# A convolution-attention hybrid on one core: an earlier second chunk, statistics beside their sums, and a reordered first tile

## The chip, the core and the metric

The kernel runs on one NeuronCore of a Trainium2 chip. A core has a matrix engine (TensorE, PE in the profile; its weight loads are PEld), a vector engine (VectorE, DVE), a scalar engine (ScalarE, ACT), a general engine (GpSimd, POOL) and a queue processor that only issues DMAs (SyncE, SP). Each works through its own instruction stream in order and waits on semaphores for the others. Matrix products land in PSUM[...]; everything else is in SBUF. The metric is the device time of one launch in microseconds (us). The comparison uses the median of several runs; the profile is one more, separate execution.

## What is computed

The input is four images of 32 x 128 x 128 in f32. Layer 0 is self-attention inside an image: the image is cut into 2 x 2 blocks, which gives 128 channels by 4096 positions, and each position attends to all the others. Layer 1 takes the result as 4 x 4096 tokens of width 128 and adds a linear attention and a routed layer of eight experts.

```python
def _L0_conv_ref(x, gamma):
    ...
    q = xs.reshape(B, C * R * R, hw)
    energy = jnp.einsum('bci,bcj->bij', q, q)
    d = jnp.sqrt(jnp.diagonal(energy, axis1=1, axis2=2))
    energy = energy / (d[:, :, None] * d[:, None, :])
    attn = jax.nn.softmax(energy, axis=-1)
    out = jnp.einsum('bcj,bij->bci', q, attn).reshape(B, C * R * R, h, w)
    out = gamma * out + xs
    ...
def _L1_attn_ref(x, Wk, Wq, Wv):
    ...
    KtV = jnp.einsum('bhnk,bhne->bhke', K, V)
    out = jnp.einsum('bhnk,bhke->bne', Q, KtV)
def _L1_ffn_ref(x, router_w, router_b, expert_w, expert_b):
    router_probs = jax.nn.softmax(x @ router_w + router_b, axis=-1)
    top_p, top_i = jax.lax.top_k(router_probs, K)
    top_p = top_p / jnp.sum(top_p, axis=-1, keepdims=True)
    expert_out = jnp.einsum('bnd,edc->bnec', x, expert_w) + expert_b
    ...
t = t + _L1_attn_ref(_ln_t(t), ...)
t = t + _L1_ffn_ref(_ln_t(t), ...)
```

So `q` is a 128 x 4096 matrix for each image, `energy` is 4096 x 4096 and symmetric, each of its columns scaled to unit length before the softmax.

## The kernel before

**The attention of layer 0.** The 4096 positions are eight chunks of 512 (`NCH`), each of four blocks of 128 (`NJ`). `attend` (from line 474) goes through the rows of chunks, i = 0 to 7, and in a row through jc = 0 to i, and for each pair through four tiles j. Only the half of the symmetric matrix up to the diagonal is computed by TensorE. A tile is: one product `pe` of two chunks of normalised positions `qn` (line 609), its exponential `pr` on ScalarE with its row sum (line 612), and two tiles later the product `po` of `pr` with the values `qT` (line 497, the function `values`). All `po` products of a row add up in one PSUM bank, the only one of its pool; after the row's last one ScalarE copies the bank to `o` (line 502).

The other half comes by transposing: VectorE turns the 32 x 32 squares of `pr` into a buffer `F` (line 421; line 565 on the diagonal), SyncE sends `F` to memory (`blocks`, line 530, or `below`, line 554) and brings it back with its groups exchanged (`swap_groups`, six DMAs, line 545). A *transposed share* (`transposed_share`, line 433, and `diagonal_share`, line 453) then multiplies `F` with the values into a `pg` bank in four steps (two on the diagonal); ScalarE takes the row sums of `F` (lines 438 and 457), and VectorE adds `pg` to `o` (lines 442 and 462). Shares wait in the list `late` with a due time on `clock`, a count of matmul work: 57 units (`LAG`) after their loads are issued. `step_share` does one step if the first of them is due. `after(n, f)` puts `f` on a list of things that are due n tiles later; `turn_tick` carries out what is due. In each tile the order is: `pe`, exponential, `turn_tick` (so also `po`), `step_share`.

**Streams beside it.** In the loop over the images (line 1496) `attend` is run as a generator that yields twice a tile. At the first of the two yields the loop collects which side streams are to move: those in `timed`, which have a begin and an end in hundredths of the image's matmul work and a number of steps, and those in `steady`, which move once in 10 clock units (`PACE`). What was collected moves at both yields. From `manual_schedule` on, the order of PE, DVE, ACT and SP is the order in which the program issues; POOL is not in that list, but instructions marked `pinned` keep their order there.

**Preparing a chunk pair.** `prep` (two chunks at a time, kc = 0 to 3) loads the pair by `load_quarters` (four DMAs on line 308, into the pool `xin`, which has one buffer) and for image 0 the same part of the token layout `T` (`load_tokens`, line 279), turns it (`turn_quarters`, line 316, two VectorE transposes for each chunk), squares and sums it (`squares`, lines 295 and 296), takes the power -0.5 on POOL (`pow_neg_half`, line 164), spreads the result (`wide`, line 388), transposes that on PE (`pnorm`, line 399) and scales `T` by it to `qn` (line 372). `prep_first` does image 0's first pair in another way: it scales the turned values (`qs`, line 338) and transposes them on PE (`ptn`, line 344); 40 idle transposes on PE (`keep_running`, line 186) run while the loads are under way.

**Layer 1.** `layer1` follows an image one image later, beside the next one's attention. `attention_rows(u)` (line 943) handles eight token groups, four instances three stream steps apart: it turns the rows, adds the attention products three at a time (`pat`, lines 855 and 920), takes the statistics of the sums (`batch_stats`, `bn_stats` on VectorE, line 962), closes them (`close_stats`: six small VectorE operations, lines 682 to 688, then on POOL the power, line 164, and two products, lines 690 and 692, the last giving `nbo`), computes the router's rows, stores the sums (`t2`, line 970) and normalises on ScalarE (line 696), which reads `nbo`. The last image does this in `last_parts` instead.

Of the kernel before, what the change touches and what calls it, by code (L numbers as in the profile page):

```python
# [12 lines left out]
F32 = mybir.dt.float32  # L13
# [3 lines left out]
ALU = mybir.AluOpType  # L17
AX = mybir.AxisListType
# [4 lines left out]
def kernel(  # L23
# [43 lines left out]
    nc = tc.nc  # L67
    P = 128
# [3 lines left out]
    CH = 512  # L72
# [228 lines left out]

    def load_quarters(b, kc, queues=(nc.sync, nc.sync)):

        xa = xin.tile([P, 2, 2, 2, HW2, 2], F32, tag="xx", name=f"xa_{b}_{kc}")
        halves = x[b].rearrange("c (s g) w -> c s (g w)", s=2)
        for a in (0, 2, 1, 3):
            first_row = 16 * kc + 4 * a
            queues[a // 2].dma_start(
                xa[ts(a, S)].rearrange("p s k r w e -> p s (k r w e)"),
                halves[:, :, first_row * W : (first_row + 4) * W],  # L310
            )
        return xa

    def turn_quarters(s, xa, qT):
        for k in range(2):
            nc.vector.transpose(
                qT[:, s, 2 * k : 2 * k + 2, :].rearrange("p h (e r c) -> p r (h e) c", e=2, r=2),
                xa[:, s, k].rearrange("p r (h t) e -> p (r h) e t", h=2),
            )

    def prep_first(st):

        b, kc = 0, 0
        st["T"] = big1.tile([P, KT, D], F32, tag="T", name="T_0")
        xa = load_quarters(b, kc, (nc.sync, nc.scalar))
        qT = chunks_of(b, kc, st)
        yield
        ss = stat.tile([P, 2 * NJ], F32, tag="ss", name=f"ss_{b}_{kc}")
        rn = stat.tile([P, 2 * NJ, 1], F32, tag="rn", name=f"rn_{b}_{kc}")
        for s in range(2):  # L330
            turn_quarters(s, xa, qT)
            squares(b, kc, s, qT, ss)
            pow_neg_half(rn[:, ts(s, NJ), 0], ss[:, ts(s, NJ)])
        keep_running(40, ps_g, "pg")
        scaled = []
        for s in range(2):
            qs = work.tile([P, NJ, P], F32, tag="qs", name=f"qs_{b}_{kc}_{s}", bufs=2)
            nc.vector.tensor_tensor(qs, qT[:, s], rn[:, ts(s, NJ)].to_broadcast([P, NJ, P]), ALU.mult)
            scaled.append(qs)
        for s, qs in enumerate(scaled):  # L340
            qn = channels(b, kc, s, st)
            pt, done = hold(f"ptn_{b}_{kc}_{s}", lambda p, qn=qn: nc.scalar.activation(qn, p, AF.Copy))  # L342
            for j in range(NJ):
                nc.tensor.transpose(pt[:, ts(j, P)], qs[:, j, :], ident)
            done()
            yield

    def prep(b, kc, st):

        ahead = 2 if b == 0 and kc == 1 else 5
        xa = load_quarters(b, kc)
        if b == 0:
            load_tokens(st["T"][:, ts(kc, 8), :], b, 8 * kc, 8)
            xx = rows_of_image(b, kc, st)
        for _ in range(ahead):
            yield
        qT = chunks_of(b, kc, st)
        for s in range(2):  # L360
            turn_quarters(s, xa, qT)
            yield
# [26 lines left out]
        yield  # L389
        if b:  # L390
            yield

# [19 lines left out]

    def after(ticks, f):
        queued.append((tick[0] + ticks, f))

    def turn_tick():

        due = [f for at, f in queued if at <= tick[0]]
        queued[:] = [q for q in queued if q[0] > tick[0]]
        for f in due:  # L420
            f()  # L421

# [51 lines left out]
    def attend(b, st):  # L474
# [11 lines left out]
        for i in range(NCH):  # L486
# [94 lines left out]
            for jc in order:  # L581
# [21 lines left out]
                for j in range(NJ):  # L603
# [11 lines left out]
                    if ending and jc == order[-1] and j == NJ - 1:  # L615
                        st["exps"] = True
                    after(2, partial(values, pr[:, c0:], t, c0, CH))
                    if jc < i and not both:
# [8 lines left out]
                    elif jc == i and j in (1, 2):  # L627

                        after(1 if j == 2 and order[-1] == i else 2, partial(below, own, (2, 1) if j == 1 else (3,)))
                    turn_tick()  # L630
                    clock[0] += 2 * (CH - c0) // P
                    step_share()
                    yield

# [19 lines left out]
    def layer1(b, st):  # L654
# [288 lines left out]
        def attention_rows(u):  # L943
# [8 lines left out]
            yield  # L952
            la = stat.tile([P, 8, 2 * E], F32, tag="la", name=f"la_{b}_{u}")
            for j0 in range(0, 8, 3):
                yield
# [3 lines left out]
                done()  # L959
            bs, stats = batch_stats("f", 8 * u, 8)  # L960
            for j in range(8):
                stats[j]()
                if j == 3:
                    yield
                    yield
            logits = router_rows(nc.vector, 8 * u, 8, la)
            close_stats("f", 8 * u, 8, bs)
            next(logits)
            yield
            nc.sync.dma_start(t2[:, ts(u, 8)], T[:, ts(u, 8), :])  # L970
            yield
# [514 lines left out]
    first, second = prep_first(states[0]), prep(0, 1, states[0])  # L1486
    next(first)
    load_weights()
    next(first)
    next(second)  # L1490
    load_tokens(states[0]["T"][:, 0:8, :], 0, 0, 8)

    ordered = ExitStack()
    ordered.enter_context(tc.manual_schedule(engines=ENGINES))
    timed = [(first, 0, 1, 2), (second, 0.5, 5.5, 10)]
    for b in range(B):
# [82 lines left out]
```

## Time and profile before

Three runs took 1643.99, 1644.94 and 1645.40 us; the median is 1644.94. The profiled execution took 1638.94 us by itself.

| | us |
|---|---|
| median of the runs | 1644.94 |
| the profiled execution | 1638.94 |
| its span, first to last instruction | 1637.1 |
| PE busy | 1598.4 |
| DVE busy | 942.7 |
| ACT busy | 877.2 |
| POOL busy | 593.8 |

The mean granted clock of TensorE is 0.996 of full speed. DMA moves 345.18 MB, 211 GB/s over the span; the share of busy time of the DMA engines lies at 0.4 to 0.7 in the first image and at 0.7 to 0.9 in the following ones.

A line of the time line gives the start, the duration from the start of the first to the end of the last of the instructions merged in it, the engine, the line of the kernel, the operation, what is written from what, the shapes and the count; in brackets stands how long the engine was idle before it, and what ended that. A line of the waits gives who waited for whom, the total in us, how many times, and the longest. The ends of matmuls are modelled: a 512-wide f32 product is two instructions that start 0.43 us apart and are shown with 0.59 us each, so two products in a row overlap in the listing, and losses are better read from starts.

The chain that ended last is PE for 84% of the span: lines 497 (25%), 609 (24%) and 433 (21%) are the three kinds of products of the attention.

### The profile page before, as it was taken

Reading aid. Unit: us, or ns where it says so; the run is one execution under the profiler, and the core shown is the slowest. Engines: PE = TensorE matmul, PEld = TensorE weight load, DVE = VectorE, ACT = ScalarE, POOL = GpSimd, SP = SyncE. Lnnn points to the kernel's source line nnn. Section 1 sums busy time; section 2 is a strip of 40 time slices with the busy share of each in tenths; the row PEclk is TensorE's granted clock in tenths of the full one; section 3 lists DMA queues with packets and bytes.
Section 4 is the critical chain, followed back from the end, with each engine's and each line's share of the span. In section 5 each row is a group of like instructions: output and inputs, shape, how many; then the busy total and the mean of one; then the engine's idle time right before and its main releaser. Section 6 shows DMA issues by size and latency. Waiting matters only on the chain.

```text
span 1637.1 us, 20938 instructions
## 1 busy us (share of the span) xinstructions
PE 1598.4 (98%) x5075; PEld 832.8 (51%) x5075; DVE 942.7 (58%) x2383; ACT 877.2 (54%) x2779; POOL 593.8 (36%) x565
## 2 busy tenths in 40 slices
PE   8999999999999999999999999999999999999887
PEld 5444444455554455555554445555554445555633
DVE  5444353468487454449468545447758644344786
ACT  3555445456465544546555554556646554555386
POOL 1000000001024442446545553156555653437166
PEclk9999999999999999999999999999999999999999
DMA  4555656675759798997898889798798989886001
GB/s 139 199 193 174 202 179 213 236 231 179 171 206 269 238 230 248 255 263 206 208 221 270 263 214 277 216 281 222 203 212 256 298 238 257 252 254 192 15 14 39
DMA packets 364728, 345.18 MB, mean 211 GB/s; under 512 B 157504, under 2 KB 291136, under 8 KB 350272
## 3 DMA queue, kind: packets, MB, share of 16 engines
q1 hardware_dynamic: 330144, 304.33, 62.1%
q0 software_dynamic: 26624, 25.58, 7.7%
q10 hardware_dynamic: 7840, 13.93, 2.9%
q8 instruction: 43, 0.70, 0.2%
q14 instruction: 77, 0.63, 0.1%
HBM read 166.90 MB, written 182.09 MB: 213 GB/s over the span
## 4 chain that ended last, share of the span: by engine, by line
PE 84%; DVE 6%; DMA 4%; ACT 2%; issue 1%; POOL 1%; SPq 1%; ACTq 0%; DVEq 0%; POOLq 0%
PE po L497 25%; PE pe L609 24%; PE pg L433 21%; PE py L1371 3%; PE pg L453 2%; DMA F<-blocks 2%; PE pys L1180 2%; PE pys L1130 2%; PE pgram L725 2%; PE pat L855 1%; SPq L545 1%; DMA below<-F 1%; PE pys L1137 1%; ACT xn L696 1%; ACT pr L612 1%
## 5 line engine op out<-in xcount | busy, mean ns | idle before, releaser
L612 ACT ACTIVATE pr<-pe 128x512 f32<-128x512 f32 (+1 forms) x576 | 322.4, 560 | 614.5 <-PE pe L609 592.1
L497 PE MATMUL po<-pr,qT 128*128 128x512 f32 (+3 forms) x1152 | 549.8, 559 | 4.2 <-ACT o L502 3.5
L609 PE MATMUL pe<-qn,qn 128*128 128x512 f32 x896 | 460.4, 596 | 4.7 <-ACT pr L612 4.7
L433 PE MATMUL pg<-F,qT 128*128 128x512 f32 x880 | 450.4, 593 | 4.6 <-DMA F<-blocks 4.6
L421 DVE STREAM_TRANSPOSE F<-pr 128x512 f32<-128x512 f32 x440 | 305.1, 700 | 167.5 <-ACT pr L612 160.1
L497 PEld LDWEIGHTS po<-pr,qT 128*128 128x128 f32 x1152 | 215.6, 191 | 251.5 <-issue 219.4
L1245 POOL DMA_INDIRECT acc<-ys,place x128 | 202.1, 1579 | 210.4 <-ACT pr L612 135.0
L438 ACT ACTIVATE junk<-F 128x512 bf16<-128x512 f32 x440 | 273.1, 621 | 5.1 <-DMA F<-blocks 5.1
L433 PEld LDWEIGHTS pg<-F,qT 128*128 128x128 f32 x880 | 166.7, 190 | 199.5 <-issue 176.2
L1066 POOL DMA_INDIRECT xs<-xn,place x192 | 185.7, 967 | 176.3 <-ACT pr L612 109.8
L609 PEld LDWEIGHTS pe<-qn,qn 128*128 128x128 f32 x896 | 158.0, 191 | 131.4 <-issue 119.2
L442 DVE TENSOR_TENSOR o<-o,pg 128x512 f32<-128x512 f32 x110 | 75.2, 683 | 244.6 <-PE pg L433 244.4
L164 POOL TENSOR_TENSOR rn<-ss,neg_half 128x8 f32<-128x8 f32 (+1 forms) x17 | 27.2, 1603 | 321.0 <-DVE ss L296 320.9
L612 ACT ACTIVATION_READ_ACCUMULATOR pr<-pe 128x1 f32 x576 | 111.8, 194 | 0.0
L609 PE MATMUL pe<-qn 128*128 128x512 f32 (+3 forms) x256 | 91.5, 440 | 0.7 <-ACT qn L342 0.7
L1245 POOL DMA_INDIRECT yb<-ys,place x64 | 61.0, 953 | 77.8 <-DMA ys<-results 47.5
L438 ACT ACTIVATION_READ_ACCUMULATOR junk<-F 128x1 f32 x440 | 84.6, 192 | 0.0
L1112 DVE TENSOR_TENSOR results<-pys,xn 128x256 f32<-128x256 f32 (+1 forms) x60 | 24.9, 416 | 83.5 <-ACT xn L1106 70.4
L164 POOL TENSOR_TENSOR rsa<-dm_a,neg_half 128x8 f32<-128x8 f32 x16 | 28.9, 1807 | 104.7 <-DVE sv_a L688 104.6
L696 ACT ACTIVATE xn<-T,nbo,rsf 128x128 f32<-128x128 f32 x128 | 54.1, 495 | 20.7 <-POOL nbo L692 20.7
L1371 PE MATMUL py<-ew_sb,xn 128*128 128x512 f32 x128 | 60.2, 610 | 5.0 <-ACT tmp L1327 3.9
L164 POOL TENSOR_TENSOR rsf<-dm_f,neg_half 128x8 f32<-128x8 f32 (+1 forms) x15 | 26.3, 1751 | 105.2 <-DVE sv_f L688 105.2
(221 smaller groups left out, 1508.0 us busy)
## 6 DMA issues: line engine op xcount, KB each, us to landing
blocks<-F SPq DMA_DIRECT2D x110, 1024.0 KB
F<-blocks SPq DMA_DIRECT2D x220, 192.0 KB
F<-blocks SPq DMA_DIRECT2D x220, 128.0 KB
F<-blocks SPq DMA_DIRECT2D x220, 64.0 KB
below<-F SPq DMA_DIRECT2D x31, 384.0 KB
T<-in_x_dram SPq DMA_DIRECT2D x64, 128.0 KB
out_dram<-acc SPq DMA_DIRECT2D x128, 64.0 KB
xa<-in_x_dram SPq DMA_DIRECT2D x62, 128.0 KB
```

Of the source, the lines that this page charges most:

```text
L164: pinned(nc.gpsimd.tensor_tensor(dst, src, neg_half.to_broadcast(list(src.shape)), ALU.pow))
L421: f()
L433: nc.tensor.matmul(pg.rearrange("p (a f) -> p a f", a=4), st["qT"][i][:, ib, :], G[:, :, ib], start=(ib == 0), stop=(ib == NJ - 1),)
L438: nc.scalar.activation(junk, G[:, :, ib], AF.Copy, accum_out=st["sums"][:, NJ * i + ib, jc : jc + 1])
L442: nc.vector.tensor_tensor(st["o"][jc], st["o"][jc], pg, ALU.add)
L497: nc.tensor.matmul(row["po"][:, lo:hi], qT[blk // NJ][:, blk % NJ, :], w, start=start, stop=(row["left"] == 0))
L609: nc.tensor.matmul(pe[:, c0:], qn[jc][:, ts(j, P)], qn[i][:, c0:], start=True, stop=True)
L612: nc.scalar.activation(pr[:, c0:], pe[:, c0:], AF.Exp, accum_out=sums[:, t, i : i + 1]).ins
L696: nc.scalar.activation(xn[:, k, :D], T[:, k, :], AF.Identity, scale=rs[:, k, :], bias=nb[:, k, :])
L1066: inst = nc.gpsimd.indirect_dma_start(xs[h], offset(place[:, i, k : k + 1]), xn[:, k, :], None)
L1245: inst = nc.gpsimd.indirect_dma_start(to, None, ys, offset(place[:, i, k : k + 1]), compute_op=op)
L1371: nc.tensor.matmul(bank, xn[:, k, :D], ew_sb[:, 4 * h : 4 * h + 4, :], start=True, stop=True)
```

## The change

The change has three parts and some that go with them.

1. *Image 0's start.* `load_quarters` can be given another place; the second pair of image 0 goes to a buffer of the pool `work` (tag `wide`) and its load is issued directly behind the first pair's. Its four quarter-transposes are handed over as a list and done one at a time between `prep_first`'s VectorE steps; the steps of `prep_first` are put in a hand-written order, with the scaled rows in another buffer (tag `grp`). The manual schedule begins earlier. The second pair's squares and power are issued before the attention begins, and what is left of its steps is timed at (1.3, 5.5, 8) instead of (0.5, 5.5, 10). The yield between the spreading and the transposes, so far only for later images, is there for image 0 too.
2. *A row's first tile.* Value products that are due at the third tile (j = 2) of a row's first pair are carried out after `step_share` instead of before it.
3. *Attention statistics.* In `attention_rows` the `bn_stats` of up to three sums follow each addition, and the statistics are closed after the last; two yields come behind that, and the store of `t2` stands one yield earlier.

```diff
-    def load_quarters(b, kc, queues=(nc.sync, nc.sync)):
+    def load_quarters(b, kc, queues=(nc.sync, nc.sync), place=(xin, "xx")):
-        xa = xin.tile([P, 2, 2, 2, HW2, 2], F32, tag="xx", name=f"xa_{b}_{kc}")
+        xa = place[0].tile([P, 2, 2, 2, HW2, 2], F32, tag=place[1], name=f"xa_{b}_{kc}")
...
+    def turn_quarter(s, k, xa, qT):
+        nc.vector.transpose(
+            qT[:, s, 2 * k : 2 * k + 2, :].rearrange("p h (e r c) -> p r (h e) c", e=2, r=2),
+            xa[:, s, k].rearrange("p r (h t) e -> p (r h) e t", h=2),
+        )
...
-        for s in range(2):
+        def rows_squared(s):
             turn_quarters(s, xa, qT)
-            squares(b, kc, s, qT, ss)
+            sq = work.tile([P, NJ, P], F32, tag="qs", name=f"sq_{b}_{kc}_{s}", bufs=2)
+            nc.vector.tensor_tensor(sq, qT[:, s], qT[:, s], ALU.mult)
+            return sq
+        def summed(s, sq):
+            nc.vector.tensor_reduce(ss[:, ts(s, NJ)], sq, AX.X, ALU.add)
             pow_neg_half(rn[:, ts(s, NJ), 0], ss[:, ts(s, NJ)])
...
+        def scale_rows(s):
+            qs = work.tile([P, NJ, P], F32, tag="grp", name=f"qs_{b}_{kc}_{s}", bufs=2)
             nc.vector.tensor_tensor(qs, qT[:, s], rn[:, ts(s, NJ)].to_broadcast([P, NJ, P]), ALU.mult)
             scaled.append(qs)
+        scaled = []
+        keep_running(40, ps_g, "pg")
+        summed(0, rows_squared(0))
+        sq = rows_squared(1)
+        st["turns"].pop(0)()
+        scale_rows(0)
+        summed(1, sq)
+        st["turns"].pop(0)()
+        st["turns"].pop(0)()
+        scale_rows(1)
+        st["turns"].pop(0)()
...
-        ahead = 2 if b == 0 and kc == 1 else 5
-        xa = load_quarters(b, kc)
+        soon = b == 0 and kc == 1
+        ahead = 2 if soon else 5
+        if soon:
+            xa = load_quarters(b, kc, place=(work, "wide"))
+            yield
+        else:
+            xa = load_quarters(b, kc)
...
-        for _ in range(ahead):
-            yield
         qT = chunks_of(b, kc, st)
-        for s in range(2):
+        if soon:
+            st["turns"] = [partial(turn_quarter, s, k, xa, qT) for s in range(2) for k in range(2)]
+            yield
+        for _ in range(0 if soon else ahead):
+            yield
+        for s in range(0 if soon else 2):
             turn_quarters(s, xa, qT)
             yield
...
-        if b:
-            yield
+        yield
...
-    def after(ticks, f):
-        queued.append((tick[0] + ticks, f))
+    def after(ticks, f, can_wait=False):
+        queued.append((tick[0] + ticks, f, can_wait))
-    def turn_tick():
+    def turn_tick(starts=False):
-        due = [f for at, f in queued if at <= tick[0]]
+        due = [q for q in queued if q[0] <= tick[0]]
         queued[:] = [q for q in queued if q[0] > tick[0]]
-        for f in due:
-            f()
+        for _, f, can_wait in due:
+            if not (starts and can_wait):
+                f()
+        return [f for _, f, can_wait in due if starts and can_wait]
...
-                    after(2, partial(values, pr[:, c0:], t, c0, CH))
+                    after(2, partial(values, pr[:, c0:], t, c0, CH), True)
...
-                    turn_tick()
+                    left = turn_tick(jc == order[0] and j == 2)
                     clock[0] += 2 * (CH - c0) // P
                     step_share()
+                    for f in left:
+                        f()
                     yield
...
+            bs, stats = batch_stats("f", 8 * u, 8)
             for j0 in range(0, 8, 3):
                 yield
                 pa, done = hold(f"pat_{b}_{u}_{j0}", partial(add_rows, u, j0, la))
                 attend_rows(u, j0, pa)
                 yield
                 done()
-            bs, stats = batch_stats("f", 8 * u, 8)
-            for j in range(8):
-                stats[j]()
-                if j == 3:
-                    yield
-                    yield
+                for f in stats[j0 : j0 + 3]:
+                    f()
+            close_stats("f", 8 * u, 8, bs)
+            yield
+            yield
             logits = router_rows(nc.vector, 8 * u, 8, la)
-            close_stats("f", 8 * u, 8, bs)
             next(logits)
-            yield
             nc.sync.dma_start(t2[:, ts(u, 8)], T[:, ts(u, 8), :])
+            yield
             yield
...
-    next(first)
-    load_weights()
+    ordered = ExitStack()
     next(first)
     next(second)
+    load_weights()
+    ordered.enter_context(tc.manual_schedule(engines=ENGINES))
+    next(second)
+    next(first)
     load_tokens(states[0]["T"][:, 0:8, :], 0, 0, 8)
-
-    ordered = ExitStack()
-    ordered.enter_context(tc.manual_schedule(engines=ENGINES))
-    timed = [(first, 0, 1, 2), (second, 0.5, 5.5, 10)]
+    next(second)
+    next(second)
+    timed = [(first, 0, 1, 2), (second, 1.3, 5.5, 8)]
```

## The prediction

> **What bounds the kernel.** I read, in this order: the busy table, the list of what TensorE (PE) waited for, and then, because PE is nearly never idle, the time line around every place where it is.
>
> ```profile
> PE 1598.4 (98%) x5075; PEld 832.8 (51%) x5075; DVE 942.7 (58%) x2383; ACT 877.2 (54%) x2779; POOL 593.8 (36%) x565
> ```
>
> PE is busy for 98% of 1637.1 us; no other engine passes 58%. The change adds no matmul, so time can only come from PE's holes. The largest waits of PE (total us, times, longest):
>
> ```profile
> PE pe L609 <- ACT pr L612: 4.7, 3, 1.6
> PE pg L433 <- DMA F<-blocks: 4.6, 3, 2.3
> PE po L497 <- ACT o L502: 3.5, 14, 0.5
> PE pnorm L399 <- DVE wide L388: 2.5, 2, 2.2
> ```
>
> Three of these four are places that the diff edits. The list counts from the modelled end of one matmul to the start of the next; the true loss is by start times. Back to back, a 512-wide f32 product (two instructions) starts 0.86 us after the one before.
>
> **Part 1, the start of image 0.** The second chunk's normalisation decides a PE stall near 20 us:
>
> ```profile
> 19.33 0.69 DVE L296 TENSOR_REDUCE ss<-sq 128x4 f32<-128x512 f32 x1
> 20.10 1.63 POOL L164 TENSOR_TENSOR rn<-ss,neg_half 128x8 f32<-128x8 f32 x1 [8.14 <-DVE ss L296]
> 21.77 0.50 DVE L388 COPY wide<-rn 128x256 f32<-128x256 f32 x2 [1.13 <-POOL rn L164]
> 22.32 1.07 PE L399 MATMUL pnorm<-ident,wide 128*128 128x128 f32 x4 [2.23 <-DVE wide L388]
> ```
>
> DVE sum, POOL power, DVE copy, PE transposes: PE stands in order behind the transposes. By start times the hole costs 2.39 us. Counting the generator's yields (each move of a timed step runs it twice, once on each half of a tile), the transposes stay at the same point of PE's order, before the third tile of row 1, while the copy moves before the second tile and the squares and the power before row 0. In VectorE's new order, with durations of the old rows (transposes 0.37, products and sums 0.65 to 0.69), the chunk's last sum ends near 15.5 us, the power (1.63) near 17.3, the copy near 17.8; PE arrives near 19.7. Two microseconds of cover: the stall goes. The four squares now stand ahead of row 0's block transposes (line 565, 0.70, 0.51 and 0.27 us), which end near 17 us as before. The scaling (four of 0.70) still has some 7 us of matmuls ahead of row 2, which reads it. What is late next there: nothing that I find.
>
> The stall has a second price:
>
> ```profile
> 19.00:22.40 3.40, 1.17 (x6) 0.51 (x5) 2.24 (x6) 1.48 (x5) 1.63 (x1) 1.00 0.32 94
> 22.40:25.80 3.40, 3.40 (x8) 1.85 (x9) 2.79 (x5) 0.67 (x2) 0.00 (x0) 0.50 0.08 24
> 25.80:28.00 2.20, 2.20 (x7) 1.00 (x6) 1.14 (x2) 0.69 (x3) 0.00 (x0) 0.99 0.00 0
> ```
>
> These are three stretches (length, then busy us of PE, weight load, DVE, ACT, POOL, then granted clock). After a stretch in which PE worked 1.17 of 3.40 us the clock was 0.50 for the next 3.4 us: 1.70 us of full-speed work lost. The Trainium skill ("TensorE: Matmul & The Clock Gate", section "Why this matters for your kernels") says that only idle gaps above about 3 us let the clock fall. By that rule a gap of 2.2 us is free and this part is worth 2.4 us; by the row it is worth 2.39 + 1.70 = **4.1 us**. I take the row.
>
> The early load costs DMA time. Four 128 KB loads go on SyncE's queue directly behind the first chunk's two, instead of at 7.50 us; two of the first chunk's four loads are on ScalarE's queue and land at 5.24. A rule speaks against that: "DMA: Bandwidth & Descriptors", section "Issuing engines are not separate DMA queues", says that DMAs of all queues interleave on the same 16 engines. By it about 60 packets of 2 KB of ScalarE's loads, outstanding when the new packets start (3.7 us), each wait for one more of about 0.1 us (packets of these loads took 84 to 107 ns): 60 x 0.1 / 16 = 0.4 us later. By the row, the T loads (512-byte packets) already share these engines in that time and the loads still land at 5.24: nothing. I take 0.2, between them. Against it, the first sum no longer stands behind the second half's transpose, as it did at 7.39 us: POOL's power starts 0.65 us earlier and the first scaled rows, at 9.58 now, start near 9.1. A chunk-2 quarter-transpose stands ahead of them and needs its load by 8.7 us. The old load had its last packets 1.5 to 2 us after its last issue; the new last issue ends near 4.6, so the load lands near 6.6, two us of cover. Net **0.25 us**, ends -0.4 and +0.5 (past 8.7 every us late would cost one). The eight T loads follow on SyncE's queue and end near 11 us; nothing reads them before 20.
>
> **Part 2, the row starts.** At a row's third tile the first value product (`po`) needs the single `po` bank, which ScalarE empties at line 502:
>
> ```profile
> 97.18 1.02 PE L609 MATMUL pe<-qn,qn 128*128 128x512 f32 x2
> 97.75 0.59 ACT L502 ACTIVATE o<-po 128x512 f32<-128x512 f32 x1
> 98.39 1.12 PE L497 MATMUL po<-pr,qT 128*128 128x512 f32 x2 [0.18 <-ACT o L502]
> 99.35 1.02 PE L433 MATMUL pg<-F,qT 128*128 128x512 f32 x2
> ```
>
> `po` should start 0.86 after `pe`, at 98.04, and starts at 98.39; `pg` follows 0.96 later instead of 0.86: 0.45 us lost. Going through the 32 evictions I find 18 such places (the wait list puts 14 under line 502; four with another releaser look the same). In 15 the loss is 0.45; in three, where row 0 of the next image begins with a 256-wide product, 0.77. In 17 of the 18 a transposed share (`pg`) follows `po` directly, as here; only 36.9 us has none. With the share first PE has 0.86 us of work while the bank empties, and that ends before `pg` does. 14 x 0.45 + 3 x 0.77 = **8.6 us**. Only `po` is delayed, and a `pr` buffer of six is held 0.9 us longer.
>
> The price: the share needs F from DMA 0.86 us earlier. From the last issue of a share's F loads to the share's first matmul I measure 5.6 to 16.7 us at the row starts concerned, and landing takes at most 3.4. Two row starts are exceptions, here the first:
>
> ```profile
> 844.85 1.02 PE L497 MATMUL po<-pr,qT 128*128 128x512 f32 x2
> 848.17 1.79 PE L433 MATMUL pg<-F,qT 128*128 128x512 f32 x2 [2.30 <-DMA F<-blocks]
> ```
>
> At 845 and 1232 us PE waits for F already; there `po` used to run inside the wait and will stand behind it: -0.86 each, -1.7. So **6.9 us**. At 1232 the clock stayed up after 1.87 us of idle; with 2.7 it may halve as it did at 848: up to -1.7 more, kept for the range.
>
> **Part 3, the statistics.** Once in each of images 1, 2 and 3 ScalarE waits for an attention group's `nbo`, and the exponentials queued behind it starve PE:
>
> ```profile
> 482.36 0.20 ACT L438 ACTIVATION_READ_ACCUMULATOR junk<-F 128x1 f32 x1
> 484.04 1.66 POOL L164 TENSOR_TENSOR rsf<-dm_f,neg_half 128x8 f32<-128x8 f32 x1 [8.26 <-DVE sv_f L688]
> 486.35 1.65 ACT L696 ACTIVATE xn<-T,nbo,rsf 128x128 f32<-128x128 f32 x4 [3.79 <-POOL nbo L692]
> 488.62 1.13 PE L609 MATMUL pe<-qn,qn 128*128 128x512 f32 x2 [1.52 <-ACT pr L612]
> ```
>
> By start times PE loses 1.84 us, and as much at 875 and 1260. The number of yields before the normalisation stays ten; closing the statistics moves from the eighth to the sixth, one tile (2.58 us) earlier. VectorE's eight `bn_stats` (0.22 each) are the same work, but four more now stand before that point, up to 0.9 us of backlog: `nbo` comes 1.7 to 2.6 us earlier. 1.84 is needed, so I count 1.7 each, **5.1 us**; the floor is 1.0 each. In images 2 and 3 POOL's gathers (1.6 us) share its order; counting halves, the power goes in before the gather that now precedes it, and that gather slips by about 2.3 us. The store of t2 goes to SyncE's queue one yield earlier, after its additions are done; it can hold F loads behind it for about its issue (0.4 us), against slacks of 5 us and more. ScalarE's remaining wait there, about 1 us, costs nothing while PE has products queued.
>
> The extra yield in image 0's later chunks shifts their transposes by half a tile, and row 4 starts some 34 us after chunk 2's scaling. Zero.
>
> **Sum.** 0.25 + 4.1 + 6.9 + 5.1 = 16.35 us. The profiled execution took 1638.94 (span 1637.1 plus 1.8 around it), so its like would take 1622.6. The unprofiled median is 1644.94 (1643.99 to 1645.4), 6.0 above the profiled one for a reason the trace can't show; I carry that over: 1644.94 - 16.35 = **1628.6 us**.
>
> **Rivals.**
> - *The statistics don't help* (0.13). VectorE is packed solid before the sixth yield, so the earlier sums arrive little earlier. For: no gap in its rows from 474 to 480. Against: only 0.9 us of work moves, for 2.6 gained. Without part 3: 1633.7.
> - *The gain is given back to DMA* (0.07). If the F loads at 848 and 1234 land when the DMA engines let them, whatever PE does, everything gained before 1234 becomes waiting there; what is left is one statistic (1.7) and one row start (0.45): 1642.8, no change. For: the chain before 848 runs through a fetch of 4.41 us and SyncE's issues. Against: these are released by steps that PE paces.
> - *Slower* (0.06). SyncE's queue waited 8.2 us for one fetch (`acc<-t`) between 780 and 850 us. If the shifted gathers put such a wait ahead of a share once in each of images 1 to 3, 24.6 us arrive against 16.35 gained: 1653.2. It decides from the point where F is issued later than 3.4 us before its share; at the tightest other row starts that takes over 2 us of delay.
> - *As worked out* (0.74): 1628.6, own range 1625 to 1633.
>
> What this kernel's measurement tells from no change is about 0.2%, 3.3 us. Faster: 0.74 + 0.13 = 0.87; same 0.07; slower 0.06. The range, 1624 to 1637, takes in the second half-clock stretch, part 3 at nothing and a few us of DMA waits; below, a start that escapes its first half-clock stretch.
>
> **What would show it.** PE's wait for `wide` gone and the clock at 1.00 from 16 to 30 us; line 502 almost gone from PE's waits; ScalarE's `nbo` waits down from 3.8 to about 1 us and PE's three waits for `pr` gone; two F waits near 3 us. I am wrong if VectorE idles near 9 us for the second chunk's load, or if F waits appear at more shares.

## The result, and the profile after

In the comparison the changed kernel takes 1638.39 us (median of 9 runs, 1633.59 to 1642.74) and the kernel before 1643.99 (9 runs, 1641.48 to 1648.91). The ratio is 0.9957, with a 95% interval of 0.9943 to 0.997: between 5 and 9 us faster. The forecast was 1628.6, a gain of 16.35. The direction was right and the size was not.

The page of the changed kernel's profile and its list of what PE waited for (who for whom; total us, times, longest) answer to the lines shown of before. The changed file is longer by some 28 lines, so 609 (`pe`) is now 637, 497 (`po`) 525, 433 (`pg`) 461, 399 (`pnorm`) 425, 502 (`o`) 530:

```profile
PE 1597.8 (98%) x5075; PEld 835.5 (51%) x5075; DVE 942.8 (58%) x2383; ACT 876.6 (54%) x2779; POOL 594.2 (36%) x565
...
PE pg L461 <- DMA F<-blocks: 8.4, 3, 3.9
PE ptd L551 <- remote: 4.7, 1, 4.7
...
PE pe L637 <- ACT pr L640: 1.6, 1, 1.6
```

Three of the four waits of before have shrunk: `pe` for `pr` from 4.7 to 1.6, `po` for `o` from 3.5 to 0.2, `pnorm` for `wide` from 2.5 to 0.3. The fourth, `pg` for its `F` from DMA, has grown from 4.6 to 8.4, and a wait of 4.7 at `ptd` is new. The span of this profile is 1636.6 us against 1637.1: taken alone, the two profiles say that nothing was gained. They mislead, and the reason is below (ScalarE's pauses).

**The start.** Time line of after, the second pair's power, its copy and PE's transposes; then windows of after (length, busy us of PE, weight load, DVE, ACT and POOL, granted clock, DMA share, GB/s):

```profile
15.71 1.63 POOL L164 TENSOR_TENSOR rn<-ss,neg_half 128x8 f32<-128x8 f32 x1 [3.77 <-DVE ss L296]
17.37 0.50 DVE L415 COPY wide<-rn 128x256 f32<-128x256 f32 x2 [0.49 <-POOL rn L164]
...
19.90 0.60 PE L425 MATMUL pnorm<-ident,wide 128*128 128x128 f32 x4
```

```profile
19.00:22.40 3.40, 3.40 (x13) 1.73 (x13) 2.50 (x4) 2.14 (x7) 0.00 (x0) 1.00 0.28 79
22.40:25.80 3.40, 3.40 (x9) 1.52 (x8) 3.09 (x7) 1.38 (x4) 0.00 (x0) 1.00 0.02 7
```

The copy starts at 17.37 us, the transposes run at 19.90 with no idle time in brackets, and the clock is 1.00 where it was 0.50.

**A row start**, time line of after. `pg` starts 0.86 us after `pe`, while the bank is still being emptied, and `po` 0.86 after that:

```profile
93.02 1.02 PE L637 MATMUL pe<-qn,qn 128*128 128x512 f32 x2
...
93.58 0.59 ACT L530 ACTIVATE o<-po 128x512 f32<-128x512 f32 x1
...
93.88 1.02 PE L461 MATMUL pg<-F,qT 128*128 128x512 f32 x2
...
94.74 1.02 PE L525 MATMUL po<-pr,qT 128*128 128x512 f32 x2
```

**The statistics**, time line of after. ScalarE still waits for `nbo`, but 1.74 us instead of 3.79, and PE's next `pe` starts without a wait:

```profile
475.17 1.66 POOL L164 TENSOR_TENSOR rsf<-dm_f,neg_half 128x8 f32<-128x8 f32 x1 [7.67 <-DVE sv_f L718]
...
477.48 1.65 ACT L726 ACTIVATE xn<-T,nbo,rsf 128x128 f32<-128x128 f32 x4 [1.74 <-POOL nbo L722]
...
478.53 1.02 PE L637 MATMUL pe<-qn,qn 128*128 128x512 f32 x2
```

**The second long F wait**, time line and windows of after. It was the one at 1232 us:

```profile
1217.02 1.02 PE L637 MATMUL pe<-qn,qn 128*128 128x512 f32 x2
1221.96 2.05 PE L461 MATMUL pg<-F,qT 128*128 128x512 f32 x2 [3.92 <-DMA F<-blocks]
1223.80 1.91 PE L525 MATMUL po<-pr,qT 128*128 128x512 f32 x2
1225.50 1.75 PE L637 MATMUL pe<-qn,qn 128*128 128x512 f32 x2
```

```profile
1220.10:1223.50 3.40, 1.54 (x2) 0.84 (x3) 0.30 (x2) 1.51 (x5) 0.83 (x1) 0.51 1.03 369
1223.50:1226.90 3.40, 3.40 (x5) 1.35 (x4) 0.00 (x0) 0.75 (x2) 0.00 (x0) 0.50 0.83 200
```

Before, PE was idle for 1.87 us here and the clock stayed up. Now it is idle for 3.92, and two windows of 3.4 us run at half clock: `po` and `pe` take 1.7 us each instead of 0.86.

### The profile page after: what moved, and what is told of

Read it like the earlier page. It is cut to its first block, busy times and chain, and to the rows that moved or that the text cites. A ratio compares the mean times of both kernels' runs of the same rounds, so it can differ in the third digit from the quotient of the medians.

```text
span 1636.6 us, 20936 instructions
## 1 busy us (share of the span) xinstructions
PE 1597.8 (98%) x5075; PEld 835.5 (51%) x5075; DVE 942.8 (58%) x2383; ACT 876.6 (54%) x2779; POOL 594.2 (36%) x565
## 4 chain that ended last, share of the span: by engine, by line
PE 88%; DVE 5%; DMA 3%; ACT 1%; issue 1%; SPq 1%; POOL 0%; another core or an unknown queue 0%; ACTq 0%; DVEq 0%
PE pe L637 26%; PE po L525 26%; PE pg L461 22%; PE py L1400 3%; PE pg L481 2%; PE pys L1209 2%; PE pat L885 1%; PE pys L1159 1%; PE pgram L755 1%; DVE df L788 1%; DMA acc<-t 1%; DMA F<-blocks 1%; PE pys L1166 1%; DVE bs_a L813 0%; PE pe_back L615 0%
## 5 line engine op out<-in xcount | busy, mean ns | idle before, releaser
L637 PEld LDWEIGHTS pe<-qn 128*128 128x128 f32 x256 | 45.2, 193 | 37.0 <-issue 33.9
```

Of the source, the lines that this page charges most:

```text
L637: nc.tensor.matmul(pe[:, c0:], qn[jc][:, ts(j, P)], qn[i][:, c0:], start=True, stop=True)
```

## The experiments

The runs come in groups (e1, e3 and e4; e5 to e8; e9 to e12; p1 to p4; q1 to q3). Those of a group share a chip and the runs of the kernel before; times of different groups are compared only through these. By "lead" I mean how much earlier the k-th matmul starts in one profile than the k-th in the other: both kernels issue 5075 in nearly the same order, so it shows at which place time is won or lost. The fill runs (e8, e12) add idle transposes whose results nothing reads; no run leaves out part of the computation.

**e1, the changed kernel again.** No edit.

> The changed kernel unaltered. The theory that its gain was partly lost by accident (ScalarE paused for 2.6 and 4.6 us near 1310 and 1502 us of the profile with its wait already met): the pauses are absent or elsewhere in this execution, and the matrix engine's lead over the profile of before is 13 to 14 us at 1117 us, about 9 after the wait for F near 1222. The rival, that the pauses belong to the changed order: they return at the same two instructions, with 2 to 5 us each. Time against before: 5 to 9 us less by the first theory's mean, by the rival the same 6 us every time.

1626.88 us against 1635.48, ratio 0.9946 (0.993 to 0.9963), with a profiled span of 1626.6. ScalarE has none of its pauses in this profile, as the first theory says. The lead over the first profile of before is 4.0 us at 28 us, 10.6 at 830, 9.4 at 860, 12.6 at 1117, 13.6 at 1215, 9.4 at 1240 and 10.5 at 1600. So 1.2 us are given back at the F wait of 838 us and 4.2 at that of 1222 us.

**e3, the statistics alone**, put into the kernel before:

```diff
+            bs, stats = batch_stats("f", 8 * u, 8)
             for j0 in range(0, 8, 3):
...
+                for f in stats[j0 : j0 + 3]:
+                    f()
+            close_stats("f", 8 * u, 8, bs)
+            yield
+            yield
```

> Before with the statistics beside their sums alone. As worked out: the three waits of the matrix engine for pr (487, 874, 1258 us) gone, 5 to 5.5 us less, F waits as before. If VectorE's backlog eats it: 0 to 2 us less.

1632.27 us against 1635.48, ratio 0.9978 (0.9969 to 0.9987). PE's three waits for `pr` are gone from its list. The lead grows by 1.84 at 877 and at 1262 us, by 1.3 at 488. By the median the gain is 3.2 us, less than the 5 to 5.5 expected: at the F wait of 1228 us PE is idle for 2.16 us, a half-clock window follows, and 2.0 us are given back.

**e4, the start alone.**

```diff
-        xa = load_quarters(b, kc)
+        soon = b == 0 and kc == 1
+        if soon:
+            xa = load_quarters(b, kc, place=(work, "wide"))
...
-    timed = [(first, 0, 1, 2), (second, 0.5, 5.5, 10)]
+    timed = [(first, 0, 1, 2), (second, 1.3, 5.5, 8)]
```

> Before with the start alone (early second chunk). As worked out: the stall at 20 us and its half-clock stretch gone, 4.1 us less, the first product at the same 11.6 us as before. If later F waits swallow a lead gained at the start: a lead of 4 us at 30 us that is gone by the end.

1632.19 us against 1635.48, ratio 0.9979 (0.9971 to 0.9987). The gain is 3.3 us where 4.1 were expected, which the interval (2.1 to 4.7) allows. The lead is 5.6 us at 28 us, some 1.5 of it a half-clock window near 12 us that this execution escaped, and still 5.6 at the end: a lead of this size passes both F waits unharmed.

**e5, the order at the row starts alone.**

```diff
-                    turn_tick()
+                    left = turn_tick(jc == order[0] and j == 2)
...
+                    for f in left:
+                        f()
```

> Before with the reordered first tile alone. If it acts as worked out: 8.6 us of row-start waits gone, the F waits at the third row's end in images 2 and 3 longer by 0.9 us each, and half-clock stretches behind them that cost up to 5 us: 2 to 6 us less than before in all, with a lead of 8 us at 1200 us. If F's arrival rules everything: no lead left at 1230 us, within 2 us of before.

On another chip 1640.31 us against 1646.1, ratio 0.9961 (0.995 to 0.9971). The lead is 7.9 us at 1280 us. PE is idle for 2.94 and 1.80 us at the two F waits, and the clock holds after both: the half-clock windows that were expected there did not come. Alone, the parts are worth 0.22, 0.21 and 0.39%, together 0.82%; in one kernel 0.38 to 0.60% in the four comparisons made. They don't add (though the third is from another chip), so something grows when they come together.

**e6, the kernel before on that chip.** No edit.

> Before unaltered, once more with a profile. If accidental pauses of an engine make the spread: the matrix engine's places of waiting are those of the first profile, and where this execution is longer, one or more pauses with the wait already met make the difference. If the first profile of before was typical: 1632 to 1640 us, and the order of waits identical within 1 us in all.

1649.66 us, span 1647.9. Against the first profile of before it has the same pace up to 1280 us (lead -0.17), and then falls to -10.7 by 1600. ScalarE stands idle there for 3 to 6 us at a time, for the most part at the same instructions as in the profile of after. These pauses are not the change's.

**e7, the order as before, in row 4 of images 2 and 3 only** (the two F waits), in the changed kernel:

```diff
-                    left = turn_tick(jc == order[0] and j == 2)
+                    left = turn_tick(jc == order[0] and j == 2 and not (b >= 2 and i == 4))
```

> The changed kernel, but in row 4 of images 2 and 3 the value product goes first again. If the longer F wait there is what was lost: the idle times there go back from 3.3 to about 2 to 2.4 us, no half-clock stretch follows at 1220, and 3 to 5 us are gained against the changed kernel. If only the order costs and not the clock: 1.7 us. If F's arrival shifts with it: nothing.

1635.57 us against 1646.1, ratio 0.9933 (0.9919 to 0.9946). In its profile the two idle times are 4.3 and 2.7 us, with half clock after both. The ratio is a little below the changed kernel's (0.994 to 0.9962), but not for the expected reason: the idle did not go back to 2 to 2.4 us, nor did the half clock at 1220 go.

**e8, idle transposes in front of the share in that row:**

```diff
+                    if b >= 2 and i == 4 and jc == order[0] and j == 2:
+                        keep_running(24, ps_e, "pe")
                     left = turn_tick(jc == order[0] and j == 2)
```

> The changed kernel with 24 idle transposes (2.6 us) ahead of the share in row 4 of images 2 and 3, so that the matrix engine works while it waits for F. If the half-clock stretches are the larger part of the loss: the share starts at the same distance from F's arrival, the clock stays at 1.0 at 838 and 1220, and 4 to 5.5 us are gained against the changed kernel. If the wait alone is the loss: no gain, or up to 1 us lost.

1638.58 us, ratio 0.9949 (0.993 to 0.9968). No window at half clock is left at 838 or 1220 us, and the longest idle is 1.5 us. `pg` starts at 838.32 and 1221.03, where it started in e1 (837.90 and 1221.25): the transposes did not hold the share up, and the half clock went. But the expected gain of 4 to 5.5 us is not in the median: it is 3.0 above e7's, and its ratio lies among those of the changed kernel.

**e9 to e12, four kernels on one chip.** First the changed kernel as the measure (e9), then the edit of e7 again (e10), a later share (e11), and a second fill (e12).

> The changed kernel, unaltered, as the measure for the three beside it on the same chip. Theory (the two long F waits, at 838 and 1222 us, cost the changed kernel more than was forecast: two half-clock windows at 1222 and longer idle): ratio 0.995, half-clock stretches after both waits, F waits of 3.3 to 3.9 us. Rival (the shortfall is a matter of one execution or chip): the ratio scatters down to 0.991, the forecast's.

e9: 1637.47 us against 1644.5, ratio 0.9962 (0.9947 to 0.9977). F waits 4.4 and 3.1; half clock after the first only, where it was expected after both. Its pauses of ScalarE come below.

> The changed kernel, but with value product before the transposed share, as in the kernel before, in row 4 of images 2 and 3 alone. Theory: PE's idle at the two waits falls by 0.86 us each (1.7 us) and at 1222 one or both of the half-clock windows go (1.7 to 3.4 us): 1.7 to 5 us less than e9, ratio 0.992 to 0.994. Rival (F's landing follows PE, so the order is worth nothing): e9's time within 0.7 us.

e10: 1636.04 us, ratio 0.9945 (0.9932 to 0.9958): 1.4 less than e9, below what was expected and within the two intervals. The idle times are 2.9 and 1.9 us; the clock held after 2.9 and halved after 1.9.

```diff
-                late.append((at or clock[0] + LAG, transposed_share(b, st, i, jc, G)))
+                more = 16 if b >= 2 and i == 3 else 0
+                late.append((at or clock[0] + LAG + more, transposed_share(b, st, i, jc, G)))
```

> The changed kernel, but transposed shares of row 3 of images 2 and 3 become due 16 units (two tiles' products, some 3.4 us of PE's work) later. Theory (PE stands at these two places because the share is put into its order before its F can have landed): both long F waits fall under 1 us together, no half-clock stretch at 838 and 1222, 8 to 11 us less than e9, ratio 0.988 to 0.990. Rival (F's loads follow PE's pace and queue, so that a later share finds its F later too, or the next shares wait instead): F waits of 2 us and more remain there or appear in rows 4 and 5, gain under 3 us.

e11: 1633.65 us, ratio 0.9926 (0.9913 to 0.9939): 3.8 less than e9, not 8 to 11, and the two intervals stand apart. The time line of this kernel at the two places:

```profile
834.19 1.02 PE L461 MATMUL pg<-F,qT 128*128 128x512 f32 x2
...
1219.08 2.03 PE L461 MATMUL pg<-F,qT 128*128 128x512 f32 x2 [3.00 <-DMA F<-blocks]
```

At 834 to 840 us no share waits and nothing runs at half clock; the lead over e9 grows there by some 5.5. At 1219 the wait of 3.0 us has stayed: SyncE issued the loads of F only from 1212.75 us, right behind four loads for layer 1 (`blocks<-rows`, 1208.09 to 1212.70), they landed at 1218.8, and that is later than the 16 units allow.

```diff
-                    left = turn_tick(jc == order[0] and j == 2)
+                    tight = b >= 2 and i == 4 and jc == order[0] and j == 2
+                    left = turn_tick(jc == order[0] and j == 2 and not tight)
+                    if tight:
+                        keep_running(20, ps_e, "pe")
```

> The changed kernel, but in row 4 of images 2 and 3 the value product comes first and 20 idle transposes follow it (they compute nothing that is used) before the share. Theory (half of the loss at the two waits is the clock's): no half-clock stretch at 838 and 1222, 3.5 to 5 us less than e9, ratio 0.992 to 0.993. Rival (the transposes delay the share by as much as the clock would cost, or the clock halves just the same): within 1 us of e9.

e12: 1637.35 us, ratio 0.9947 (0.9934 to 0.9959), e9's time, as the rival said. The clock did what the theory expected. Time line and windows of this kernel at the first place:

```profile
838.12 1.10 PE L461 MATMUL pg<-F,qT 128*128 128x512 f32 x2 [0.45 <-DMA F<-blocks]
```

```profile
835.00:838.40 3.40, 2.96 (x23) 2.45 (x22) 2.00 (x7) 0.73 (x3) 2.23 (x2) 1.00 0.94 333
838.40:841.80 3.40, 3.40 (x10) 1.50 (x9) 0.00 (x0) 3.40 (x12) 0.67 (x1) 1.00 0.96 209
```

That won 3.2 us on e9 at the first place and 0.2 at the second, where e9 had kept its clock anyway. Among ScalarE's pauses between 1400 and 1515 us this execution then falls behind e9 by 5.5. So neither fill run shows the clock's share in its time; it is read from the profiles, place by place.

**p1 to p4, two profiles of each kernel on one chip**, to compare them by place without pauses or with the same.

> The kernel before, looked at once more beside the changed one on one chip. Open: the changed kernel leads by 11 to 14 us at 1280 us and its medians by 6 to 9 only, and between 1280 and 1520 us ScalarE stands idle for 3 to 6 us at a time with what it waits for already there, in some profiles of both kernels. Theory (the pauses take the same from both kernels): this kernel loses 6 to 11 us of pace between 1280 and 1520 us against its first profile, as it did once before. Rival (they are the changed kernel's own, and the earlier look an exception): at most 2 us.

> The changed kernel, beside the kernel before on one chip. Theory (pauses alike in both): 6 to 11 us lost between 1280 and 1520 us, and 11 to 14 us ahead of the kernel before at 1280 us and still at the end, where both have the same clock at the start. Rival (the pauses take more from the changed kernel): it gives back 3 us and more of its lead there against the kernel before on this chip.

> The kernel before once more on this chip, to see how far two profiles of one kernel differ between 1280 and 1520 us. Theory: within 3 us of the other look. Rival: the pauses are a matter of the single execution, and differ by 5 us and more.

> The changed kernel once more on this chip: as for its first look here. The mean of the two against the mean of the kernel before tells what of the lead at 1280 us is left at the end: theory 11 us and more, rival 6 to 9 us.

The kernel before took 1638.37 (p1) and 1637.13 us (p3), the changed one 1627.84 (p2) and 1627.15 (p4). None of the four has a pause between 1280 and 1520 us, so this is the clean comparison: 10.25 us gained, a lead of 10.24 at the end. (It doesn't answer what the pauses take from each kernel where they occur.) The share at the first F wait in p1 and in p2:

```profile
848.18 1.12 PE L433 MATMUL pg<-F,qT 128*128 128x512 f32 x2 [2.08 <-DMA F<-blocks]
```

```profile
838.40 2.05 PE L461 MATMUL pg<-F,qT 128*128 128x512 f32 x2 [3.82 <-DMA F<-blocks]
```

The second F wait in p1 and in p4:

```profile
1231.58 1.02 PE L497 MATMUL po<-pr,qT 128*128 128x512 f32 x2
1233.91 1.10 PE L433 MATMUL pg<-F,qT 128*128 128x512 f32 x2 [1.31 <-DMA F<-blocks]
```

```profile
1216.04 1.02 PE L637 MATMUL pe<-qn,qn 128*128 128x512 f32 x2
1220.07 2.04 PE L461 MATMUL pg<-F,qT 128*128 128x512 f32 x2 [3.00 <-DMA F<-blocks]
1221.90 1.91 PE L525 MATMUL po<-pr,qT 128*128 128x512 f32 x2
1223.61 1.91 PE L637 MATMUL pe<-qn,qn 128*128 128x512 f32 x2
```

The mean lead, place by place (means of the two profiles of each kernel):

| place | forecast, us | measured, us |
|---|---|---|
| start of image 0 (up to 28 us) | 0.25 + 4.1 | 4.40 |
| statistics, three places | 5.1 | 5.41 |
| row starts and small things between | 8.6 | 7.92 |
| the two F waits | -1.7 | -7.49 |
| sum | 16.35 | 10.24 |

These are two profiles of each kernel. Over all four of before and all six of the changed kernel without an edit, the two F waits cost the changed kernel 5.5 us more than before, and the start is worth 3.5: the first and the fourth row hold some chance.

**q1 to q3, the later share once more** (q2), with the changed kernel (q1) and the order of e7 (q3) beside it.

> The changed kernel, unaltered, as the measure for the two beside it. Theory (the two F waits with their clock cost 7.2 us of PE's pace where 1.7 was forecast): F waits of 3 to 4 us at 838 and 1222 us with one or two half-clock windows each. Rival (an accident of some executions): one of the two places is without.

q1: 1626.41 us against 1635.92, ratio 0.994 (0.9927 to 0.9954). F waits 4.1 and 3.3; two windows at half clock after the first, one after the second.

> The changed kernel, with the shares of row 3 of images 2 and 3 due 16 units later, a second time and against the changed kernel in the same call. Theory: the wait at 838 us gone, the one at 1222 us left at about 3 us as before, 3 to 5 us less than the changed kernel's median. Rival (the first look was luck): within 1.5 us.

q2: 1624.23 us, ratio 0.9927 (0.9914 to 0.9941): 2.2 less than q1, a miss. The wait at 838 us is gone and some 7 us are won by there; some 2 are given back near 1490 us, where PE waits for ScalarE's `xn` in front of `pgram`, and 1.2 in a half-clock window at 1555 us that q1 doesn't have.

> As q2, and in row 4 of images 2 and 3 the value product first, as in the kernel before. Theory (the order costs 0.86 us where PE waits for F, and the clock where the idle passes some 2 us): 0.5 to 2.5 us less than q2. Rival (with the share due later the bank is empty in time and the order is worth nothing, or costs 0.45 us): q2's time within 0.5 us, or slower.

q3: 1623.43 us, ratio 0.9928 (0.9914 to 0.9941): 0.8 less than q2, which these runs can't tell from nothing. The later share gives the best versions tried: 11 to 12.5 us under the kernel before in two groups, and 2 to 4 under the changed one (with intervals of the ratios that stand apart in e9 to e12 and overlap in q1 to q3).

## Why the prediction was wrong

**The start, right in its mechanism, with some luck in the number.** 4.35 forecast, 4.40 measured. The early load's net of 0.25 measured 0.3 at 18 us in these pairs, and 0.03 between the two first profiles: there the loads land 0.25 us later, the power starts 0.14 earlier, not 0.65, and the first scaled rows start at 9.59 us, not near 9.1, since a quarter-transpose of the second pair stands ahead of them. The 1.70 of the clock were counted in full. Both p1 and p3 have the half-clock window behind the stall, so the pairs show it in full; of six profiles with the old start two (e3, e6) don't have it, and none of the fourteen with the new start has it. On average that is some 1.1 us.

**The row starts, right.** Each of the 14 places with 0.45 and the three with 0.77 appears in the lead with that size. The 0.7 missing in the table are a longer F wait at 180 us (0.17) and 0.3 each at 764 and 1151 us.

**The statistics, right.** 1.8 us each, where 1.84 was the whole loss and 1.7 was counted. The rival that they don't help falls with e3.

**The two F waits, wrong.** This is the step that failed: "there `po` used to run inside the wait and will stand behind it: -0.86 each, -1.7", with "up to -1.7 more, kept for the range". The wait and its direction were right; its size was not. In p1 to p4 it cost 7.5 us, in two terms, both mis-sized:

- *Idle.* In the four profiles PE's idle before the share grew from 1.8 to 3.95 us at 838 (means of 2.08, 1.54 and of 3.82, 4.08) and from 1.56 to 3.04 at 1222 (1.31, 1.80 and 3.08, 3.00): 3.6 us, not 1.7. Of each, 0.86 is the order; the rest is that F came 1.3 and 0.6 us late against PE's lead. The share starts earlier than before by 10.05 us where PE had a lead of 11.34, and by 11.15 where it had 11.78. That is the rival of a gain given back to DMA, in a small dose: F follows PE, but not all the way. The chain of work in front of the share shows both. It starts with a fetch (`acc<-t`) that a step of PE releases; from there over SyncE's issues to the share it takes 9.2 us before and 10.8 after at 838, and 9.3 and 9.9 at 1222.
- *Clock.* The remaining 3.9. The two profiles of after have six windows at half clock at these places, the two of before have one. Each is 1.7 us of full-speed work, so 5 x 1.7 / 2 = 4.3 at most, and a little less since part of the first window is idle.

Over all ten profiles of the two kernels both terms are there but smaller: the idle grows by 1.45 and 1.6 us at the two places (means), and a profile of after has 2.7 half-clock windows there where one of before has 1.0, which makes some 2.8 us. That is 5.9 by this count and 5.5 by the lead, against 1.7 forecast.

I had the clock's price in the right size and the condition wrong. One gap of 2.2 us with half clock behind it and one of 1.87 without looked like a threshold, and at 1232 I left the case out of the sum. The rule below gives it three chances in four at an idle of 3.0, and certainty from 3.8. The rule of the Trainium skill that I had set aside ("TensorE: Matmul & The Clock Gate", section "Why this matters for your kernels": gaps above about 3 us) points at these two places, with idle of 3.0 to 4.1, but not at 20 us, where 1.9 us of idle (p1) and 2.5 (p3) did halve the clock, and 2.5 in e3 and e6 did not: neither it nor one row gives the condition. The same page's section "What's actually happening" has the half that both lack, a window that runs free of the kernel, and I didn't use it.

**Carrying 6.0 us over from profile to median, wrong in kind.** The profiled execution of before has no pauses of ScalarE. Medians of before are 1635.5 and 1635.9 us on two chips whose profiles (of whatever kernel) show none, and 1644.5 and 1646.1 on two whose profiles show them. So the median of 1644.94 probably holds pauses and its profile didn't; that was not shown, since no run here gives both for the same execution. What follows for the gain: 8.6 and 9.5 us in the medians on chips without pauses, 10.2 between profiles, and 5.6 (the comparison above) and 7.0 (e9) where the profiles show pauses. So of the 10.75 us by which the comparison missed the forecast, the two F waits explain 4 to 6; the 4.6 between 10.2 and 5.6 come beside the pauses. Why less is gained there is open: one profile of before lost 10.6 us after 1280 us (e6), two of the changed kernel 10.3 and 10.5 (e9, after), and other versions of it 8 to 16.

SyncE's queue, the slower rival, put nothing ahead of any other share: in the changed kernel's list F is waited for at three places, 180, 838 and 1222 us.

## What to carry to other kernels

Where an engine already waits for data, list these places first. A consumer that is put earlier there adds its step to the wait, and of the gains made ahead of the place that part which the data don't follow (here 5 to 11%). A change that lengthens a gap of TensorE from under 1.9 us to over it can buy a half-clock window too, so a few microseconds of gap have a price step. Giving the consumer a later due time won 5 to 7 us at one place here (2 to 4 in the median), more than undoing the order did in e10 and q3. And before two profiles are compared, look for idle stretches that the program doesn't cause: here one of the two had 10 us of them.

## What the runs showed of the hardware

**The clock is set on a grid of 3.413 us.** In each of 20 profiles the half-clock windows start at distances that are whole multiples of 3.413 us to within 0.01 (in after: 837.8 - 11.8 = 242 of them, 1220.1 - 837.8 = 112), and the grid lies differently in each execution. The Trainium skill says so too ("TensorE: Matmul & The Clock Gate", section "What's actually happening": a free-running window of 3413 ns); new is how idle a window has to be. Between 20 and 1500 us, a window behind one at full clock ran at half when PE had been busy for less than about 1.5 us in the one before: in all 30 cases the busy time was 1.51 or less, and before the some 8600 windows that stayed at full clock it was never below 1.51. Seven further half-clock windows followed on another one, with 1.6 to 2.7 us busy at half speed there, which is 0.8 to 1.4 of work; where 2.8 and more was busy, the clock came back. Busy times are modelled, and the border is not a law: at the start and after 1500 us, where short products and transposes fill PE's time, 10 of 36 half-clock windows followed on 1.56 to 2.28 us of busy time, and some windows with 1.6 to 1.9 did not lead to one.

For a gap in a dense stretch this gives an estimate. A window of 3.41 us needs 3.41 - 1.51 = 1.90 us of idle. So a gap below 1.9 us doesn't halve the clock by itself; a gap g between 1.9 and 3.8 does it with a chance of about (g - 0.4) / 3.4, by where it lies on the grid; a longer one always. That is why 1.9 us of idle halved it in e10, and 2.9 in the same run did not. All six gaps of 3.8 us and more at the F waits had half clock behind them.

**Transposes count.** Twenty idle transposes (2.35 us) in front of a share kept the clock at 1.00 at both F waits (e12), and 24 did in e8. In e12 PE would have worked for about 1.2 us of the window at 838 without them (an estimate from its time line), less than the 1.5.

**ScalarE's pauses.** The time line of the changed kernel on a chip with pauses (e9), and of the same instruction on one without (p2):

```profile
1309.99 1.02 PE L637 MATMUL pe<-qn,qn 128*128 128x512 f32 x2
...
1310.65 0.19 ACT L466 ACTIVATION_READ_ACCUMULATOR junk<-F 128x1 f32 x1
...
1316.65 0.60 ACT L640 ACTIVATE pr<-pe 128x512 f32<-128x512 f32 x1 [5.81 <-PE pg L461]
...
1317.39 1.12 PE L637 MATMUL pe<-qn,qn 128*128 128x512 f32 x2 [2.09 <-ACT pr L640]
```

```profile
1311.98 1.02 PE L637 MATMUL pe<-qn,qn 128*128 128x512 f32 x2
1313.04 0.60 ACT L640 ACTIVATE pr<-pe 128x512 f32<-128x512 f32 x1 [1.28 <-PE pe L637]
```

The exponential at 1316.65 is that of the `pe` which starts at 1309.99 and ends near 1311.0 (both are the 510th of their kind), 6.7 us later; on the other chip the same one follows 1.1 us after its `pe`'s start. Such pauses come between 1270 and 1520 us, for the most part at the same instructions of ScalarE in both kernels, cost 8 to 16 us there, and appear on some chips only. No run here shows what they wait for.
